# Layer 1's query projection as seven block products for eight, and another order for the slot

## The chip, the core and the metric

The kernel runs on one core of a Trainium2 chip as one launch. The metric is device time in microseconds of that launch, from several runs; one more execution was taken by the hardware profiler. PE is TensorE (PEld its weight loads), DVE VectorE, ACT ScalarE, POOL GpSimd, SP the engine whose queue issues most DMA transfers.

## What is computed

Two transformer layers with adaptive layer norm, on x of 2 x 512 x 512 (two batches b, 512 tokens, width 512), all in fp32. Layer 0 is a sliding-window attention and a low-rank-adapted FFN; layer 1 a latent attention with 128 heads and a routed FFN. The part that is changed is in layer 1's attention:

```python
    q_c = (c_q @ Wq_up).reshape(b, s, N_HEADS, HEAD_DIM)        # 4 per head
    q_r = (x @ Wq_rope).reshape(b, s, N_HEADS, ROPE)            # 64 per head; 512 x 8192 weights
    ...
    scores = (einsum('bqhd,bkhd->bhqk', q_c, k_c) + einsum('bqhd,bkd->bhqk', q_r, k_r)) / scale
    attn = softmax(scores)
    out = einsum('bhqk,bkhd->bqhd', attn, v_c)
    out = out.reshape(b, s, N_HEADS * HEAD_DIM) @ Wo
```

## The kernel before

Layer 0 comes first (to about 920 us of the profiled execution). Its loop runs over 64 steps, four for each of 16 units (8 key-value groups times 2 batches). In each step stand, in an order written out by hand, the scores of one block of 128 queries, the band and maximum on DVE, the exponentials on ACT, the normalisation on POOL, and block products for the next and the last unit. Layer 0's own query and output projections are already block products of half size (`ps_q` at L856, `pw` at L1002: 128x256 instead of 128x512). Into the steps is put, one piece a step, a list `aside`: the modulation rows of both layers, 21 pieces.

Layer 1's attention is a loop of 64 **slots**. A slot t is one of `quads`: a group g of 16 heads (of 8), a batch b, and a quarter s of the group; four heads as two pairs p = 0, 1. What a slot does:

- `query` (L1296): q of one pair of heads, `psq` = 128 rows (2 heads x 64) x 512 tokens, four matmuls over the input width; weights `wqr`, one 512 KB load per slot. `query_out` (L1306, ACT) copies it to SBUF.
- `inner`, `inner_hi`, `inner_parts` (L1315, L1326, L1333): the latent queries or keys of two slots; `own_query` (L1355) masks them for one pair, on POOL for p = 0 and on DVE for p = 1.
- `rope` (L1363, L1372): scores of one pair for 128 keys (block i of 4), `s`, 64-row matmuls, two heads side by side. `keep` (L1382, ACT) copies them to SBUF, `largest` (L1389, DVE) keeps the running maximum.
- `blocks`, `tops`, `twice`, `join`, `top`, `top_hi`, `top_lo`, `stripes`: the maximum over keys for each query, ending on POOL (L1432). `row` h (L1442) spreads it over 128 partitions with one 64-row matmul for each of the four heads into `psm`: heads 0 and 1 from partitions 0 to 63, heads 2 and 3 from 64 to 127. `row_copy` and `row_even` (L1454, L1458, ACT) take three of the four to SBUF.
- `less_even`, `less_odd` (L1463, L1465, L1469): the maximum subtracted; four on DVE straight from PSUM (head 0), twelve on POOL. `exponential` (L1472, ACT).
- `own_values` (POOL) and `mix` (L1518, PE): attention times values, 32-column matmuls into `acc`.
- `extra`, `extra_dve`, `extra_pool`: what is due once in four slots or so: values `psv`, the division `psb`, the output projection `psw`.

The order of all this is a table, `PLAN1`: each entry names an operation, its arguments and an offset in slots, and the loop issues them in that order; every engine takes its instructions in the order of issue. The tiles `psq`, `psu`, `psx`, `psm`, `psv`, `psb` and `psw` share three PSUM banks in rotation (`pX`); `s` has one buffer for each pair, `acc` one. After the loop `tail()` lists the last slot's rest and the FFN by hand; the dictionary `beside` places pieces of the FFN in the last slots.

Of the kernel before, what the change touches and what calls it, by code (L numbers as in the profile page):

```python
# [45 lines left out]
def adaln_kernel(ctx: ExitStack, tc: tile.TileContext, A: dict, out: bass.AP):  # L46
# [89 lines left out]
    def spread_gates(L, ws, g, pool, dst):  # L136

        n = 32 * len(ws)
        for i, s in enumerate(ws):
            for b in range(B) if s in dst else ():  # L140
                r = 32 * i + b
                ps = pool.tile([P, 512], F32, tag="mm", name=f"psg{L}_{s}_{b}")
                nc.tensor.matmul(
                    ps, lhsT=ident[:n, r : r + 1].to_broadcast([n, P]), rhs=g, start=True, stop=True
                )
                nc.scalar.copy(dst[s][b], ps)
# [138 lines left out]
    class Ffn1:  # L285
# [3 lines left out]
        def __init__(self, cp, wp, ap, pS, pX):  # L289
            self.cp, self.wp, self.ap, self.pS, self.pX = cp, wp, ap, pS, pX  # L290
            self.mv, self.rstd, self.xn, self.pl, self.pr, self.ps, self.hw = ({} for _ in range(7))
            self.wT, self.gate, self.gb = [], [], []
# [30 lines left out]
        def weight(self):  # L323

            h = len(self.wT)
            w = self.wp.tile([P, 2, D], F32, tag="wq", name=f"wT1_{h}")
            src = A["L1_ffn_WT"].rearrange("(kc p) o -> p kc o", p=P)
            nc.sync.dma_start(out=w, in_=src[:, 2 * h : 2 * h + 2, :])
            self.wT.append(w)

        def routes(self):
            nc.vector.tensor_copy(self.em, self.em_i)
            r = self.cp.tile([LAT, NH * HD1], F32, tag="wv", name="route")
            self.route = r[:N1, : E1 * R]
            nc.vector.tensor_scalar(self.route, self.erow, self.em, None, ALU.is_equal)

        def gates(self, b):
# [4 lines left out]
                lhsT=ident[:64, 32 + b : 33 + b].to_broadcast([64, P]),  # L342
# [4 lines left out]
            g = self.ap.tile([P, D], F32, tag=f"q{b}", name=f"g1_5_{b}")  # L347
# [3 lines left out]
        def low_weights(self):  # L351
            a = self.ap.tile([P, D], F32, tag="q0", name="aT1")
            self.aT = a.rearrange("p (kc e) -> p kc e", kc=KC)
            nc.sync.dma_start(out=self.aT, in_=A["L1_ffn_AT"].rearrange("(kc p) e -> p kc e", p=P))
            self.bT = self.ap.tile([P, D], F32, tag="q1", name="bT1")
# [174 lines left out]

    with ExitStack() as c01:
        mid = c01.enter_context(tc.tile_pool(name="mid", bufs=1, side="right"))
        gate = {2: gate_tiles(0, 2, state), 5: gate_tiles(0, 5, mid)}
        grow = [
            pool.tile([64, D], F32, tag=f"grow{L}", name=f"grow{L}")
            for L, pool in enumerate((mid, state))
        ]
        scs = [silu_c(L, mid) for L in range(2)]
        with ExitStack() as c00:
# [96 lines left out]
            def reload(t):  # L636
# [10 lines left out]
                ],  # L647
# [17 lines left out]
        attention1(tc, A, small, hT, xs, gate[2], ident, normalised, c01.close, Ffn1)  # L665
# [79 lines left out]
def attention0(  # L745
# [383 lines left out]
    tops 1 -2; extra_pool 1 -1; keep 0 0 -1; twice -2; keep 3 1 -2; join -2; own_query 1 0;  # L1129
    own_query 0 0; exponential 1 1 -3; rope 1 0 -1; respread -4; top -2; rope 0 1 -1; top_hi -2;  # L1130
    exponential 1 2 -3; top_lo -2; stripes -2; query_out 0 0; less_odd 1 3 -3; keep 0 1 -1;
    mix 1 -3; extra 0 0; row 3 -2; largest 1 0 -1; row 1 -2; keep 1 0 -1; rope 1 1 -1;
    row_copy 0 -2; rope 2 0 -1; extra_dve 0 0; own_values -2; row_copy 1 -2; row 2 -2;
    largest 1 1 -1; extra_pool 0 0; exponential 1 3 -3; less_odd 0 2 -2; row 0 -2;
    largest 2 0 -1; keep 1 1 -1; extra 1 0; less_even 0 2 -2; less_even 0 0 -2; mix 2 -3;
    keep 2 0 -1; less_odd 0 0 -2; mix 3 -3; less_odd 1 2 -2; row_even -2; rope 2 1 -1;
    rope 3 0 -1; inner -1; less_odd 1 0 -2; less_odd 0 3 -2; less_even 0 1 -2; less_even 1 0 -2;
    less_even 0 3 -2; largest 2 1 -1; exponential 0 2 -2; exponential 0 0 -2; inner_hi -1;
    largest 3 0 -1; keep 2 1 -1; less_even 1 1 -2; leave -3; extra_dve 1 0; less_odd 0 1 -2;
    keep 3 0 -1; query 1 1; inner_parts -1; blocks 0 -1; less_odd 1 1 -2; tops 0 -1;  # L1140
    exponential 1 0 -2; less_even 1 2 -2; rope 3 1 -1; exponential 0 3 -2; query_out 1 1;
    exponential 0 1 -2; less_even 1 3 -2; rope 0 0 0; largest 3 1 -1; mix 0 -2; query 0 1;
    blocks 1 -1;
# [3 lines left out]
def attention1(tc, A, small, hT, xs, ga, ident, normalised, close, ffn):  # L1147
# [17 lines left out]
    with ExitStack() as ctx:  # L1165
# [3 lines left out]
        def load_q(t):  # L1169
            g, _, s = quads[t]  # L1170
            w = wp.tile([P, KC, 2 * P], F32, tag="wq", name=f"wqr{t}")
            c0 = (4 * g + s) * 2 * P
            nc.sync.dma_start(out=w, in_=wqr[:, :, c0 : c0 + 2 * P])
            return w
# [35 lines left out]
        wv = cp.tile([LAT, NH * HD1], F32, tag="wv", name="wv")  # L1210
# [5 lines left out]
        wqs = {}  # L1216

        with ExitStack() as c:
# [28 lines left out]
            wqs[0] = load_q(0)  # L1247
            for b in range(B):
                normalised(b, pmm)
                for n, w in zip(names, downs):  # L1250
# [13 lines left out]
                    if n != "kr":  # L1264
                        nc.scalar.copy(hi[b][n], f)
                        nc.vector.tensor_sub(lo[b][n], f, hi[b][n].bitcast(F32))

# [7 lines left out]
        chain, later, last = [], [], []  # L1275
        todo = {(e, i): [] for e in ("dve", "pool") for i in range(2)}
# [15 lines left out]
        def query(t, pair):  # L1292
            b = quads[t][1]
            ps = hold["q", t, pair] = pX.tile([P, S], F32, tag="x", name=f"psq{t}_{pair}")
            for kc in range(KC):
                nc.tensor.matmul(  # L1296
                    ps,
                    lhsT=wqs[t][:, kc, pair * P : (pair + 1) * P],
                    rhs=hT[b][:, kc, :],
                    start=(kc == 0),  # L1300
                    stop=(kc == KC - 1),
                )

        def query_out(t, pair):
            q = qs[t, pair] = ap.tile([P, S], F32, tag=f"q{pair}", name=f"q{t}_{pair}")
            nc.scalar.copy(q, hold["q", t, pair])  # L1306

        def inner(t):
# [4 lines left out]
            ps = hold["u", n, i] = pX.tile([P, S], F32, tag="x", name=f"psu{n}_{i}")  # L1313
# [16 lines left out]
        def inner_parts(t):  # L1330
# [9 lines left out]
            )  # L1340

# [7 lines left out]
        def own_query(t, p):  # L1349
# [4 lines left out]
            e = nc.vector if p else nc.gpsimd  # L1354
            e.tensor_scalar_mul(c, src, cols[:, x : x + 1])  # L1355
# [54 lines left out]
        def join(t):  # L1410
            ps = hold["x", t] = pX.tile([P, P], F32, tag="x", name=f"psx{t}")
            nc.tensor.transpose(ps, ms[t].rearrange("p a b c -> p (a b c)"), ident)

        def top(t):
# [3 lines left out]
            nc.vector.tensor_reduce(m, src, AX.X, ALU.max)  # L1418

# [10 lines left out]
        def stripes(t):  # L1430
            m = hold["st", t] = ap.tile([P, 16, 32], F32R, tag="st", name=f"st{t}", bufs=2)
# [6 lines left out]
        def row(t, h):  # L1438

            ps = hold["m", t, h] = pX.tile([P, S], F32, tag="x", name=f"psm{t}_{h}")  # L1440
# [9 lines left out]
        def row_copy(t, p):  # L1450
# [3 lines left out]
            nc.scalar.copy(r, hold["m", t, 2 * p + 1])  # L1454

        def row_even(t):
            r = hold["r", t, 2] = ap.tile([P, S], F32, tag="rowe", name=f"rowe{t}", bufs=2)
            nc.scalar.copy(r, hold["m", t, 2])  # L1458

        def less_even(t, p, i):  # L1460
# [3 lines left out]
            else:  # L1464
                nc.vector.tensor_sub(s, s, hold["m", t, 2 * p])  # L1465
# [8 lines left out]
        def values(t):  # L1474
# [3 lines left out]
            def product():  # L1478
                ps = pX.tile([P, TB, 64], F32, tag="x", name=f"psv{t}")
# [10 lines left out]
            def copy(ps):  # L1490
                v = vcs[g, b] = ap.tile([P, TB, 64], F32, tag="v", name=f"v{t}")
                nc.vector.tensor_copy(v, ps)

# [32 lines left out]
        def leave(t):  # L1526
# [30 lines left out]
            def spreading():  # L1557
                ps = pX.tile([P, S], F32, tag="x", name=f"psb{g}_{b}")
# [3 lines left out]
            def scale(ps):  # L1562
# [4 lines left out]
                )  # L1567

# [3 lines left out]
            def project(i):  # L1572
                ps = pX.tile([P, 512], F32, tag="x", name=f"psw{G}_{b}_{i}")
# [5 lines left out]
            def gated(i, ps):  # L1579
                y = ap.tile([P, D], F32, tag="y", name=f"y1_{G}_{b}_{i}", bufs=2)  # L1580
                nc.vector.tensor_mul(y, ps, ga[b])
                return y
# [37 lines left out]
        def extra_pool(t, i):  # L1620
# [7 lines left out]
            for f in (  # L1628
                query, query_out, inner, inner_hi, inner_parts, respread, own_query, rope,
# [17 lines left out]
        F = ffn(cp, wp, ap, pS, pX)  # L1647
# [16 lines left out]
        beside = {  # L1664
# [245 lines left out]
```

## Time and profile before

| | us |
|---|---|
| runs | 2483.36 median of 3 (2481.84 to 2483.59) |
| the profiled execution | span 2480.0, its run 2481.8 |
| layer 0 and the start of layer 1 | 0 to about 920 |
| slots | about 920 to 2380 |
| last FFN | to 2480 |

Busy over the whole span: PE 97%, PEld 52%, DVE 74%, ACT 57%, POOL 71%. The stages differ, and the shares are to be read stage by stage. In the rows of the profile a group is named by line, engine, operation and tiles; "128*128" is the shape of PE's array that a matmul uses, "64*128" one half of its rows, "128*32" a quarter of its columns. A fp32 matmul shows as two instructions (two passes), one of type fp32r as one. A PE length includes some 0.16 us of pipeline, so that lengths overlap; what a pass costs is read from the distance of the starts.

### The profile page before, as it was taken

What the parts mean: (1) busy time and instruction counts of PE and PEld (TensorE: products, weight loads), DVE (VectorE), ACT (ScalarE), POOL (GpSimd) and SP (SyncE); (2) the same over time, 40 slices, a digit from 0 to 9 for tenths busy, and PEclk for the clock granted to TensorE, in tenths of its full rate; (3) what the DMA queues carried; (4) which work ended last, traced back from release to release, by engine and by line L of the source; (5) the groups of instructions that cost most, each with busy time, mean ns of one, the idle gap of its engine ahead of it and who ended that gap; (6) DMA issues with size and microseconds to landing.
All of it is one profiled execution on the core that took longest, in us unless ns stands there. A gap on an engine that the chain in (4) does not pass through costs nothing.

```text
span 2480.0 us, 31453 instructions
## 1 busy us (share of the span) xinstructions
PE 2403.0 (97%) x11516; PEld 1278.4 (52%) x11516; DVE 1827.2 (74%) x2464; ACT 1419.0 (57%) x2128; POOL 1763.1 (71%) x1659
## 2 busy tenths in 40 slices
PE   6999999999999999999999999999999999999878
PEld 4677777777776543444444344444344434444333
DVE  4666777777788347777787788778877777788764
ACT  1232222222222127888888788878888888888640
POOL 2555567557577325888898888888988898888743
PEclk8999999999999999999999999999999999999978
DMA  6212101100101100000000100000000000010000
GB/s 215 73 48 81 41 14 33 43 14 31 35 5 39 45 11 26 26 26 26 26 18 26 30 19 25 26 26 26 22 27 26 26 18 26 30 33 18 18 9 34
DMA packets 79845, 83.14 MB, mean 34 GB/s; under 512 B 7885, under 2 KB 69100, under 8 KB 79692
## 3 DMA queue, kind: packets, MB, share of 16 engines
q1 hardware_dynamic: 79548, 81.00, 10.5%
q8 instruction: 91, 1.49, 0.3%
q14 instruction: 62, 0.51, 0.1%
q0 software_dynamic: 144, 0.15, 0.0%
HBM read 79.03 MB, written 2.10 MB: 33 GB/s over the span
## 4 chain that ended last, share of the span: by engine, by line
PE 91%; DVE 5%; POOL 2%; ACT 1%; issue 1%; DMA 0%; SPq 0%; DVEq 0%; POOLq 0%; ACTq 0%
PE s L1363 19%; PE psq L1296 18%; PE acc L1518 10%; PE ps_q L856 7%; PE pw L1002 7%; PE s L1372 5%; PE po L951 4%; PE scores L898 2%; PE ps_k L797 2%; PE pt L940 2%; PE psv L811 2%; PE psu L1315 2%; PE psm L1442 2%; PE psw L1574 1%; PE psf L505 1%; PE psf L270 1%
## 5 line engine op out<-in xcount | busy, mean ns | idle before, releaser
L1469 POOL TENSOR_TENSOR ss<-ss,row 128x512 f32<-128x512 f32 x504 | 635.1, 1289 | 42.5 <-ACT row L1454 42.5
L1382 ACT COPY ss<-s 128x1024 f32<-128x1024 f32 x512 | 505.4, 1015 | 177.2 <-PE s L1372 130.6
L1363 PE MATMUL s<-q,ckr 64*128 64x512 f32 x2048 | 554.9, 612 | 10.5 <-ACT ss L1382 10.5
L1472 ACT ACTIVATE ss<-ss 128x1024 f32<-128x1024 f32 x512 | 525.2, 1070 | 5.7 <-DVE ss L1684 4.6
L1296 PE MATMUL psq<-hT,wqr 128*128 128x512 f32 x1024 | 467.2, 598 | 0.0
L1372 PE MATMUL s<-qm,c 64*128 64x512 f32 x1024 | 419.3, 795 | 0.4 <-DVE c L1333 0.4
L1389 DVE TENSOR_TENSOR mx<-s,mx 128x1024 f32<-128x1024 f32 x256 | 306.7, 1219 | 40.2 <-PE s L1372 39.2
L1463 POOL TENSOR_TENSOR ss<-ss,rowe 128x512 f32<-128x512 f32 x252 | 318.5, 1288 | 0.0
L1296 PEld LDWEIGHTS psq<-hT,wqr 128*128 128x128 f32 x1024 | 188.9, 189 | 241.0 <-issue 210.4
L1363 PEld LDWEIGHTS s<-q,ckr 64*128 64x128 f32 x2048 | 184.2, 186 | 215.1 <-ACT ss L1382 97.1
L1518 PE MATMUL acc<-ss,vp 128*32 128x512 f32 x2048 | 266.1, 612 | 0.0
L790 POOL TENSOR_TENSOR qT<-t_q,t_q 128x512 f32<-128x512 f32 x64 | 82.0, 1281 | 234.8 <-DVE t_q L789 234.8
L1389 DVE TENSOR_TENSOR mx<-s,ss 128x1024 f32<-128x1024 f32 x128 | 156.7, 1225 | 116.7 <-ACT row L1454 80.6
L942 ACT COPY pT<-pt 128x512 f32<-128x512 f32 x64 | 37.6, 587 | 229.7 <-PE pt L940 229.7
L1432 POOL TENSOR_TENSOR st<-mh,own_block 128x512 fp32r<-128x512 f32 x64 | 67.0, 1047 | 142.8 <-DVE mh L1428 142.8
L1372 PEld LDWEIGHTS s<-qm,c 64*128 64x128 f32 x1024 | 104.7, 187 | 119.0 <-issue 114.9
L1394 DVE STREAM_TRANSPOSE mx<-mx 128x1024 f32<-128x1024 f32 x128 | 158.8, 1241 | 2.3
L1400 DVE TENSOR_REDUCE m<-mx 128x32 f32<-128x1024 f32 x128 | 156.1, 1220 | 4.4
L1465 DVE TENSOR_TENSOR ss<-ss,psm 128x512 f32<-128x512 f32 x252 | 155.7, 680 | 0.0
L1355 POOL TENSOR_SCALAR qm<-c,cols 128x512 fp32r<-128x512 f32 x64 | 102.6, 1603 | 44.0 <-PE s L1372 24.7
L931 POOL TENSOR_TENSOR p<-p,rs 128x512 f32<-128x512 f32 (+1 forms) x64 | 108.6, 1697 | 26.8 <-DVE rs L930 22.6
L1518 PEld LDWEIGHTS acc<-ss,vp 128*32 128x32 f32 x2048 | 47.5, 109 | 138.0 <-issue 106.7
(249 smaller groups left out, 3906.1 us busy)
## 6 DMA issues: line engine op xcount, KB each, us to landing
wqr<-in_L_attn_Wq_rope_pairs SPq DMA_DIRECT2D x64, 512.0 KB
wmod<-in_L_wmod SPq DMA_DIRECT2D x20, 512.0 KB
wq<-in_L_attn_wq SPq DMA_DIRECT2D x8, 1024.0 KB
wo<-in_L_attn_wo SPq DMA_DIRECT2D x32, 256.0 KB
wmod<-in_L_wmod SPq DMA_DIRECT2D x2, 1024.0 KB
x<-in_L_attn_x SPq DMA_DIRECT2D x8, 256.0 KB
wk<-in_L_attn_wk SPq DMA_DIRECT2D x8, 256.0 KB
wv<-in_L_attn_wv SPq DMA_DIRECT2D x8, 256.0 KB
```

Source lines behind the costliest of these rows:

```text
L856: nc.tensor.matmul(ps[:, j, :], lhsT=s[:, k, j * P : (j + 1) * P], rhs=t[:, k, :], start=(k == 0), stop=(k == 1),)
L1002: nc.tensor.matmul(ps[:, j, :], lhsT=s[:, hh, j * P : (j + 1) * P], rhs=t[:, hh, :], start=(hh == 0), stop=(hh == 1),)
L1296: nc.tensor.matmul(ps, lhsT=wqs[t][:, kc, pair * P : (pair + 1) * P], rhs=hT[b][:, kc, :], start=(kc == 0), stop=(kc == KC - 1),)
L1363: nc.tensor.matmul(out[:, j, :], lhsT=whole[b]["kr"][r, bass.ts(i, P)], rhs=qs[t, p][r, :], start=True, stop=False,)
L1372: nc.tensor.matmul(out[:, j, :], lhsT=qkc[t // 2, 1][r, bass.ts(i, P)], rhs=qm[t, p][r, :], start=False, stop=True,)
L1382: nc.scalar.copy(ss[t, i, p], hold["s", t, i, p])
L1389: nc.vector.tensor_max(mx[t, p], hold["s", t, i, p], before)
L1394: nc.vector.transpose(m, m)
L1463: nc.gpsimd.tensor_sub(s, s, hold["r", t, 2])
L1469: nc.gpsimd.tensor_sub(s, s, hold["r", t, 2 * p + 1])
L1472: nc.scalar.activation(ss[t, i, p], ss[t, i, p], AF.Exp)
L1518: nc.tensor.matmul(accs[g, b][32 * h : 32 * (h + 1), :], lhsT=vps[t][:, kb, h, :], rhs=ss[t, kb, h // 2][:, h % 2, :], start=(s == 0 and k ...
```

## The change

The query projection of a slot, 256 outputs x 512 inputs times 512 x 512 tokens, is cut in 2 x 2 blocks and done as seven products of 128 x 256 x 256 (Strassen's scheme in Winograd's form). What it needs:

- Sums of weight blocks, S1, S2 and S4, for each of the 32 (g, s). `blending` makes them in layer 0 as 33 more pieces of `aside`, one a step: a 512 KB load, one DVE add of 128x512, two POOL adds of 128x256, and a 512 KB store into DRAM (`blended`, which holds a fourth, the unused first quarter, too).
- Sums of token blocks, once for each (g, b), `combine` on POOL (three of 128x512) into `part0` to `part2`; one more subtraction is made in place in hT at the start of layer 1.
- `product` j = 0 to 3 in place of `query`: one, two, two and two block products, each 2 matmuls of 128x256. Weights come as seven loads of 128 KB a slot into a ring of eight, each issued after the product that used its place.
- `sums` i = 0 to 5 in place of `query_out`: an ACT copy of 128x256, two DVE operations of 128x512, three of 128x256, each reading PSUM and SBUF.

`own_query` 0 goes from POOL to ACT. `PLAN1` is a new table; among others, the rows 1 and 0 now stand together, with row 2 and row 3 each between two `rope` entries of a pair, and both `extra` entries stand next to products 0 and 1. `stripes` and `row_even` have one buffer for two. `beside` is a list that also waits for a bank to be free; some operations of the last slots are left out of the loop since `tail()` issues them. The layer-1 gate rows, Wv_up and the routing table share one tile, and the FFN's weights go into the ring of the query weights.

```diff
+        def blend(i):
+            w = held.pop().rearrange("p k (r n) -> p r k n", r=2)
+            a11, a12 = (w[:, 0, 2 * k : 2 * k + 2, :] for k in range(2))
+            o = pool.tile([P, KC, DH], F32, tag="wmod", name=f"bo{i}", bufs=2)
+            _, s1, s2, s4 = (o[:, j, :].rearrange("p (k n) -> p k n", k=2) for j in range(KC))
+            nc.vector.tensor_add(
+                o[:, :2, :].rearrange("p j (k n) -> p j k n", k=2),
+                w[:, :, :2, :],
+                w[:, 1, :, :].rearrange("p (j k) n -> p j k n", j=2),
+            )
+            nc.gpsimd.tensor_add(s2, s1, a11)
+            nc.gpsimd.tensor_add(s4, s2, a12)
+            if i + 1 < len(blended):
+                load(i + 1)
+            nc.sync.dma_start(out=blended[i], in_=o)
...
-                ],
+                ] + blending(tmp),
...
-        def load_q(t):
-            g, _, s = quads[t]
-            w = wp.tile([P, KC, 2 * P], F32, tag="wq", name=f"wqr{t}")
...
+        def load_q(n):
+            t, k = divmod(n, 7)
...
+            nc.sync.dma_start(out=wq[:, n % 8, :, :], in_=src)
...
-        def query(t, pair):
-            b = quads[t][1]
-            ps = hold["q", t, pair] = pX.tile([P, S], F32, tag="x", name=f"psq{t}_{pair}")
-            for kc in range(KC):
-                nc.tensor.matmul(
...
+        def combine(t, j):
+            b = quads[t][1]
+            if quads[t][2] == 0:
+                nc.gpsimd.tensor_tensor(
+                    parts[j],
+                    parts[0] if j else quarter(b, 0, 1),
+                    quarter(b, (0, 1, 1)[j], (0, 1, 0)[j]),
+                    ALU.add if j else ALU.subtract,
+                )
+
+        def product(t, j):
+            b = quads[t][1]
+            ps = hold["q", t, j] = bank([P, 2, DH], f"psq{t}_{j}")
+            rhs = (
+                (quarter(b, 0, 0),),
+                (quarter(b, 1, 0), parts[0]),
+                (parts[1], quarter(b, 0, 1)),
+                (quarter(b, 1, 1), parts[2]),
+            )[j]
+            n = 7 * t + max(2 * j - 1, 0)
+            for i, r in enumerate(rhs):
+                for k in range(2):
+                    nc.tensor.matmul(
+                        ps[:, i, :],
+                        lhsT=wq[:, (n + i) % 8, k, :],
+                        rhs=r[:, k, :],
+                        start=(k == 0),
+                        stop=(k == 1),
+                    )
+            for m in range(n, n + len(rhs)):
+                if m + 8 < 7 * NQ:
+                    load_q(m + 8)
...
+            if i == 0:
+                nc.scalar.copy(q[:, 3, :], ps[:, 0, :])
+            elif i == 1:
+                nc.vector.tensor_add(q[:, 0::3, :], q[:, 3:4, :].to_broadcast([P, 2, DH]), ps)
+            elif i == 2:
+                nc.vector.tensor_sub(q[:, 1:3, :], q[:, 3:4, :].to_broadcast([P, 2, DH]), ps)
+            elif i == 3:
+                nc.vector.tensor_sub(q[:, 3, :], ps[:, 1, :], q[:, 1, :])
+            elif i == 4:
+                nc.vector.tensor_add(q[:, 1, :], q[:, 1, :], ps[:, 0, :])
+            else:
+                nc.vector.tensor_sub(q[:, 2, :], ps[:, 1, :], q[:, 2, :])
...
-            e = nc.vector if p else nc.gpsimd
-            e.tensor_scalar_mul(c, src, cols[:, x : x + 1])
+            if p:
+                nc.vector.tensor_scalar_mul(c, src, cols[:, x : x + 1])
+            else:
+                nc.scalar.mul(c, src, cols[:, x : x + 1])
```

The new table, with what bears on PE's order and the banks in it:

```diff
+    extra 1 0; rope 0 0 -1; rope 0 1 -1; less_even 1 0 -3; combine 1 0; own_values -2; twice -2;
...
+    exponential 0 2 -3; sums 2 0; own_query 1 0; rope 1 0 -1; rope 1 1 -1; sums 3 0; largest 1 0 -1;
+    exponential 1 2 -3; keep 1 0 -1; row 1 -2; row 0 -2; largest 1 1 -1; mix 2 -3; rope 2 0 -1;
+    row_copy 0 -2; keep 1 1 -1; less_even 1 3 -3; row 2 -2; rope 2 1 -1; extra_pool 1 -1;
+    exponential 1 3 -3; less_even 0 1 -2; combine 0 1; combine 2 0; keep 2 0 -1; less_even 0 3 -2;
+    largest 2 0 -1; largest 2 1 -1; mix 3 -3; keep 2 1 -1; row_even -2; extra_pool 0 0;
+    less_odd 0 3 -2; less_odd 0 0 -2; less_even 0 2 -2; less_even 0 0 -2; rope 3 0 -1; row 3 -2;
+    row_copy 1 -2; keep 3 0 -1; rope 3 1 -1; largest 3 0 -1; inner -1; inner_hi -1; less_odd 0 1 -2;
+    keep 3 1 -1; product 3 0; exponential 0 0 -2; blocks 0 -1; product 0 1; inner_parts -1;
+    sums 4 0; sums 5 0; less_odd 1 1 -2; largest 3 1 -1; less_even 1 1 -2; blocks 1 -1; product 1 1;
+    tops 1 -1; extra 0 0; leave -3; exponential 0 3 -2; sums 0 1; exponential 1 1 -2;
+    less_odd 1 0 -2; respread -1; tops 0 -1;
```

In the table of before, `row 3` and `row 1` stand together, and so do `row 2` and `row 0`.

## The prediction

> **What bounds the kernel now.** I read the busy time by stretch first, then PE's (TensorE's) order inside the stretch that holds the change, then the rows of the single operations. Durations are those of one profiled execution: span 2480.0 us, its run 2481.8, which is 1.6 below the median of the runs, 2483.36. The sum is made against 2481.8, and 1.6 is added at the end. About 0.2% (5 us) is what a measurement of this kernel can tell from no change.
>
> Busy time by stretch; the columns are the stretch, its length, busy us (and instructions) of PE, PEld, DVE, ACT and POOL, the clock, DMA:
>
> ```profile
> 0.00:920.00 920.00, 883.62 (x4524) 643.88 (x4525) 636.84 (x898) 210.17 (x686) 507.06 (x390) 0.99 0.15 48
> 1000.00:2300.00 1300.00, 1299.99 (x6150) 539.69 (x6148) 1026.34 (x1340) 1082.32 (x1290) 1123.67 (x1144) 1.00 0.08 25
> 2300.00:2480.00 180.00, 143.81 (x525) 61.67 (x523) 113.35 (x162) 73.30 (x90) 89.68 (x82) 0.85 0.05 18
> ```
>
> From 1000 to 2300, the loop over layer 1's slots, PE is busy 1299.99 of 1300 us at full clock; the others are at 79 to 86%. The stretch holds 58 slots (the once-a-slot rows count x58), so a slot takes 22.41 us, and it is as long as its PE work. The waits of PE in this stretch come out empty.
>
> PE's order in one slot (start, length of each merged group), and in layer 0 a run of passes half as wide:
>
> ```profile
> 1409.74 3.60 PE L1296 MATMUL psq<-hT,wqr 128*128 128x512 f32 x8
> 1413.27 1.13 PE L1363 MATMUL s<-q,ckr 64*128 64x512 f32 x4
> ...
> 1423.76 0.50 PE L1442 MATMUL psm<-st,own_head 64*128 64x512 f32 x2
> 1424.10 1.02 PE L1363 MATMUL s<-q,ckr 64*128 64x512 f32 x4
> ...
> 1426.28 0.39 PE L1442 MATMUL psm<-st,own_head 64*128 64x512 f32 x2
> 1426.60 1.92 PE L1518 MATMUL acc<-ss,vp 128*32 128x512 f32 x16
> ```
>
> ```profile
> 376.48 3.72 PE L856 MATMUL ps_q<-th,s 128*128 128x256 f32 x16
> 380.04 1.04 PE L940 MATMUL pt<-ident,p 128*128 128x128 f32 x8
> ```
>
> The eight 512-wide query passes hold PE from 1409.74 to 1413.27, 3.53 us. The single starts lie 0.429 apart, and the last step is 0.52 because the next group has another array shape (64 rows). A fp32 matmul is two passes, so a slot has 16 of these. In layer 0 sixteen 256-wide passes take 3.56 us, starts 0.216 apart and 0.10 more once. A change of array shape (128 rows; 64 rows; 32 columns) thus costs about 0.1 on leaving and 0.1 on the first pass after. The psm rows come in pairs: one pass in the lower 64 rows and one in the upper run together, 0.34 and 0.32 us a pair.
>
> **The change, part by part.**
>
> *Products (PE).* 16 passes of 0.429 = 6.86 us become 7 block products x 2 matmuls x 2 passes = 28 of 0.216 = 6.05. That is -0.82 a slot, times 64 = **-52.2 us**. The half-wide price is a row of this kernel, same shape and type, so I take it as it stands. Each pass also loads weights (PEld 0.189): under 0.216 it still hides, as it does in layer 0.
>
> *Row passes (PE).* The new order table issues psm 1 and psm 0 together, then psm 2 and psm 3 alone, each between two s groups. Rows 0 and 1 both sit in the lower 64 rows, 2 and 3 in the upper. So nothing is left to run as a pair: four passes one after the other, where there were two pairs. A pass is about 0.217 (a pair's 0.32 less a change), so +0.43 a slot; 63 slots use the table: **+27.3 us**. Bounds: 0 if the chip overlaps them with neighbours after all, 27.3 if not. I take 27.3, since an s group uses both halves.
>
> *Array changes (PE).* Counting along the built order of PE from the first s to the last table row, before has 602 changes of array shape, after 562: psw and psb now stand beside the query products instead of between psm and acc. 40 x 0.195 = **-7.8 us**. Counted this way (passes times step, plus changes), before gives 996.6 us over 44 slots where the trace has 992.7, so the counting itself is good to 0.4%.
>
> At one place a page speaks against all this. The Trainium skill, "TensorEngine Tiling (Array Packing)", section Instruction Overhead, gives each matmul some 60 cycles of overhead. At a clock of 2.4 GHz, which "TensorE: Matmul & The Clock Gate" states in its table, an estimate is 25 ns a pass, for 12 more passes +0.3 us a slot and +19 us in all, which would leave a gain of only 14. The trace disagrees: 0.216 against half of 0.429 is under 2 ns.
>
> *Reading the products (DVE, ACT).* Two ACT copies of psq (588 ns each, L1306) go; a 128x256 copy comes (a 64x256 copy from PSUM took 365). DVE gets five reads of PSUM plus SBUF: two 128x512 (0.68, the L1465 row) and three 128x256. These have no row: bounds 0.36 (half, and a little) and 0.68; I take 0.42, as the 128x256 copy at L1492 took 425. Together 2.6 us (at most 3.4). DVE has 1026.34/58 = 17.7 a slot; it comes to 20.3 (21.1) of 21.9. Its cover is thus 1.6 (0.8) us a slot: PE hides it, barely.
>
> ```profile
> L1465 DVE TENSOR_TENSOR ss<-ss,psm x232: 676/680/684, 1002.3 to 2282.5; 128x512 f32<-128x512 f32 x116
> ```
>
> ```profile
> L787 DVE TENSOR_TENSOR t_q<-qT,rope x51: 692/693/1753, 107.1 to 696.2; 128x512 f32<-128x512 f32 x51
> ```
>
> (ns, least/median/most.) The first has one operand in PSUM and never varies, with POOL 86% busy beside it. The second reads SBUF twice and sometimes takes 1.75. All five new reads are of the first kind.
>
> *POOL and ACT.* own_query 0 (1603 ns, L1355) goes from POOL to ACT, where a scaled 128x512 takes some 690 (L1326). POOL gets three combines of 1.29 per four slots, 0.97 each. POOL: 19.4 - 1.6 + 1.0 = 18.8 a slot; ACT: 18.7 - 1.18 + 0.37 + 0.69 = 18.6. Both under 21.9: 0.
>
> *The bank that is closest.* Three PSUM banks rotate over ten tiles a slot. psu takes the bank of psm 0, which is free after the fourth less_even on DVE. From the end of product 2, DVE has in its order: sums 2, own_query 1, sums 3, two largest, two less_even, two largest, two less_even = 0.62+0.5+0.36+2.28+1.24+2.28+1.24 = 8.5 us (steps between starts). PE, up to psu: two s groups 2.28, psm 0.53, acc 1.0, s 1.19, psm 0.22, s 1.19, acc 1.0, s 1.19, psm 0.22, s 1.19 = 10.0. DVE is 1.5 us early. Cost 0; with the cover gone, 64 us for each us late.
>
> *Weights.* 64 loads of 512 KB become 448 of 128 KB on SP, each waiting for the product eight loads back, about a slot ahead. Behind them in SP stand only the wo loads, needed slots later. DMA is at 0.08. Cost 0.
>
> *Layer 0.* 32 steps each get a load, a DVE add 128x512 of the L787 kind (0.69 to 1.75), two POOL adds 128x256 (about 0.64 each), and a store. DVE's add stands just before the band add, where DVE waited for PE 0.2 to 0.8 us, 0.5 on average. POOL is 63% busy. On SP the next load waits for POOL's second add; queued behind are wo, wk, wv and wq loads, which already waited long for their buffers:
>
> ```profile
> SPq L709 <- PE pw L1002: 251.9, 22, 54.0
> ```
>
> PE has no idle time here, but slack: t_q at 463.6 gave qT by 464.8, for scores at 467.4. Bounds: 0, and 32 x (1.75-0.5) = 40 us. I take **+3**.
>
> *Start and end of layer 1.* The in-place subtraction and first combine (2 x 1.29 on POOL) lie beside 12 matmuls, 10.3 us of PE. The tail is the same code: psf weights wait for the last product, some 70 us ahead of use. 0, within 3 either way.
>
> Sum: -52.2+27.3-7.8+3 = -29.7; 2481.8-29.7+1.6 = **2453.7**.
>
> **Rivals.**
> (1) *The row passes cost nothing*: -27.3 more, 2426. For it: pairs do overlap. Against: the halves don't fit. If only psm 2 and 3 hide, 2440.
> (2) *DVE gives its banks back late* (slower). Place: psu behind the fourth less_even. Price 64 us per us beyond 1.5; it decides no change from 2.0 late (1.5+0.5 gained). Two collisions of the 1.75 kind per slot (2 x 1.05 = 2.1) plus three reads at the upper bound on the way (+0.3) make 2.4: +58 us, 2511. Against: the L1465 row.
> (3) *Layer 0's covers are gone*, +40 instead of 3: 2490. For it: PE is at 100% there too, and DVE's new add is of the colliding kind. Against: 0.5 of wait in front of it.
> (4) *Something outside these*, start or tail, 2453 +- 30.
>
> **How the numbers follow.** Forecast 0.67 (2440 to 2470, faster). (1) 0.07, faster. (2) 0.14: 0.02 faster, 0.02 same, 0.10 slower, since it may be mild. (3) 0.08: 0.04, 0.02, 0.02. (4) 0.04: 0.01, 0.01, 0.02. Faster 0.81, same 0.05, slower 0.14. The range, 2438 to 2486: the low end leaves out rival 1 in full, the high end takes in most of (3) and leaves out (2).
>
> **What would show it.** PE still at 1300 of 1300 in the slots and a slot near 21.9; 0.216 steps in psq; single psm passes of 0.2 to 0.3; DVE near 92%; L1465's kin at 0.68. Wrong if PE waits on less_even, sums or inner_parts; if layer 0 ends later than before by more than 5 us; or if psm adds nothing.

## The result, and the profile after

The changed kernel takes 2718.24 us (median of 4 runs, 2716.68 to 2718.81); the kernel before took 2482.7 beside it. The ratio is 1.0948, 95% interval [1.0929, 1.0967]: slower by 235.5 us, where 29.7 faster was forecast. The profiled execution has a span of 2714.9 us, 234.9 more than before's.

Where the time went is read from two tiles that start once in a fixed place. The first line of each pair is the first weight product of layer 1 (its first start ends layer 0), the second the turn of the score maxima, once a slot. Before, then after:

```profile
L1253 PE MATMUL pscq<-hT,L_attn_Wq_down x16: 592/592/697, 889.1 to 909.7; 128*128 128x512 f32 x16
L1412 PE MATMUL psx<-ident,m x64: 272/273/476, 951.2 to 2374.0; 128*128 128x128 f32 x64
```

```profile
L1299 PE MATMUL pscq<-hT,L_attn_Wq_down x16: 592/592/697, 930.1 to 951.5; 128*128 128x512 f32 x16
L1517 PE MATMUL psx<-ident,m x64: 327/328/476, 991.4 to 2605.1; 128*128 128x128 f32 x64
```

Layer 0 ends 930.1 - 889.1 = 41.0 us later. From the first psx to the last it is 1613.7 us for 1422.8: 190.9 more in 63 slots, 3.03 a slot. From layer 1's start to the first psx it is 61.3 for 62.1, and from the last psx to the end 109.8 for 106.0. The four differences, 41.0, 190.9, -0.8 and 3.8, make 234.9. In the steady part (psx 10 to 58) a slot is 25.49 us, before 22.52; where a slot is named below, it is this one.

Busy time by stretch, the columns as in the prediction:

```profile
0.00:920.00 920.00, 854.96 (x4405) 628.38 (x4406) 642.20 (x891) 201.07 (x668) 555.09 (x437) 0.98 0.26 85
1100.00:2400.00 1300.00, 1160.58 (x6033) 596.61 (x6033) 1050.86 (x1442) 936.65 (x1136) 966.83 (x1000) 1.00 0.12 37
```

In layer 0 PE has 855.0 us in the first 920, where it had 883.6. In the slots, where it was busy 1299.99 of 1300 us, it now is 1160.58, at full clock; DVE is at 81%, ACT at 72, POOL at 74. No engine is the bound. So the slot is a chain of waits from engine to engine. PE's waits in that stretch, which came out empty before (us in total, times, longest):

```profile
PE s L1468 <- ACT ss L1487: 74.5, 101, 1.1
PE s L1468 <- DVE mx L1494: 39.5, 52, 0.8
PE psq L1374 <- DVE c L1435: 23.3, 51, 0.5
```

PE starts a new score tile s late because ACT's copy of the last one (keep, L1487) or DVE's maximum over it (largest, L1494) is late. The groups of these two say why; the last part of each line is the idle time ahead of them and what ended it:

```profile
L1487 ACT COPY ss<-s 128x1024 f32<-128x1024 f32 x409 | 412.0, 1020 | 353.0 <-DVE mx L1494 229.8 <-PE acc L1630 123.2
L1494 DVE TENSOR_TENSOR mx<-s,mx 128x1024 f32<-128x1024 f32 x206 | 246.8, 1219 | 198.7 <-ACT ss L1487 198.7
```

ACT stands 229.8 us for DVE, and DVE 198.7 us for ACT, over a tile that both only read. Before, the same two groups waited for PE:

```profile
L1382 ACT COPY ss<-s 128x1024 f32<-128x1024 f32 x464 | 457.9, 1015 | 147.3 <-PE s L1372 113.9 <-PE acc L1518 17.7 <-DVE mx L1389 15.7
L1389 DVE TENSOR_TENSOR mx<-s,mx 128x1024 f32<-128x1024 f32 x232 | 278.0, 1219 | 37.3 <-PE s L1372 36.2
```

The instruction order of the two programs shows what these waits are. An instruction's waits stand at its end; these are largest 2 0 on DVE before, then largest 2 0 on DVE and keep 2 1 on ACT after (slot numbers left out of the names). PE_49, DVE_49 and Activation_49 are the counters that PE, DVE and ACT raise as they finish instructions:

```
L1389 TensorTensor mx_0_8300<-s_2_0_8313,mx_0_8300 128x1024 [waits PE_49]
L1494 TensorTensor mx_0_8841<-s_2_0_8856,mx_0_8841 128x1024 [waits DVE_49,Activation_49]
L1487 TensorCopy ss_2_1_14836<-s_2_1_14820 128x1024 [waits DVE_49,Activation_49]
```

The count of ACT that largest 2 0 waits for is the one that keep 2 0 of the same tile brings, and the count of DVE that keep 2 1 waits for is that of largest 2 1; the other counter in each line is the engine's own. So the program has two engines read one score tile in turns, in the order in which the table issues them. Before's table always has largest ahead of keep. After's has keep ahead at tiles 2 0, 3 0 and 3 1 and largest ahead elsewhere. With one tile for each p, PE's next scores wait for both readers, one after the other. One slot in the timeline of DVE (start, length, and the wait in brackets):

```profile
1505.25 2.36 DVE L1494 TENSOR_TENSOR mx<-s,mx 128x1024 f32<-128x1024 f32 x2 [2.01 <-ACT ss L1487]
1507.52 1.28 DVE L1573 TENSOR_TENSOR ss<-ss,psm 128x512 f32<-128x512 f32 x2
1510.63 1.22 DVE L1494 TENSOR_TENSOR mx<-s,mx 128x1024 f32<-128x1024 f32 x1 [1.83 <-ACT ss L1487]
```

The copies of ACT and the score groups of PE beside them:

```profile
1504.19 1.02 ACT L1487 COPY ss<-s 128x1024 f32<-128x1024 f32 x1
1507.69 1.01 ACT L1487 COPY ss<-s 128x1024 f32<-128x1024 f32 x1 [2.48 <-DVE mx L1494]
```

```profile
1506.53 1.13 PE L1468 MATMUL s<-q,ckr 64*128 64x512 f32 x4 [0.76 <-DVE mx L1494]
1508.76 1.13 PE L1468 MATMUL s<-q,ckr 64*128 64x512 f32 x4 [0.64 <-ACT ss L1487]
```

ACT copies tile 2 0 from 1504.19 to 1505.21; only then does DVE read it (1505.25), and PE's scores 3 0 begin at 1506.53. DVE's maximum of 2 1 ends at 1507.61; only then does ACT copy it (1507.69), and PE's scores 3 1 begin at 1508.76. The wait passes from DVE to PE, to ACT and back to PE within 5 us, which is why no busy share is high.

Layer 0's loss is another wait, DVE's longest in 300 to 700 (us in total, times, longest):

```profile
DVE bo L551 <- DMA bl<-bo: 49.4, 15, 6.5
```

DVE's sum of one step waits until the store of the step before has landed, up to 6.5 us, and everything behind it on DVE is late. In one such step DVE's sum begins at 404.92, POOL reaches its second add only at 417.07, SP issues the store at 418.24, and DVE's next sum begins at 425.10, after 6.27 us of waiting.

### The profile page after: what moved, and what is told of

Same layout as the page of the kernel before. It is cut to its first block, busy times and chain, and to the rows that moved or that the text cites. A ratio compares the mean times of both kernels' runs of the same rounds, so it can differ in the third digit from the quotient of the medians.

```text
span 2714.9 us, 34328 instructions
## 1 busy us (share of the span) xinstructions
PE 2436.4 (90%) x12284; PEld 1435.3 (53%) x12284; DVE 2035.5 (75%) x2816; ACT 1401.2 (52%) x2128; POOL 1791.2 (66%) x1709
## 4 chain that ended last, share of the span: by engine, by line
PE 40%; DVE 28%; ACT 16%; issue 8%; POOL 6%; DMA 3%; SPq 0%; DVEq 0%; ACTq 0%; POOLq 0%
ACT ss L1487 11%; DVE mx L1494 9%; PE psq L1374 7%; PE ps_q L889 4%; DVE mx L1499 4%; PE acc L1630 4%; PE s L1468 4%; PE pw L1035 3%; DMA bl<-bo 2%; ACT row L1560 2%; PE po L984 2%; PE ps_k L830 2%; DVE q L1400 1%; DVE c L1435 1%; DVE m L1505 1%
## 5 line engine op out<-in xcount | busy, mean ns | idle before, releaser
L1487 ACT COPY ss<-s 128x1024 f32<-128x1024 f32 x512 | 515.6, 1020 | 437.2 <-DVE mx L1494 287.1
L1468 PE MATMUL s<-q,ckr 64*128 64x512 f32 x2048 | 569.6, 627 | 143.5 <-ACT ss L1487 92.7
L1494 DVE TENSOR_TENSOR mx<-s,mx 128x1024 f32<-128x1024 f32 x256 | 306.7, 1219 | 242.6 <-ACT ss L1487 242.6
L1468 PEld LDWEIGHTS s<-q,ckr 64*128 64x128 f32 x2048 | 171.3, 185 | 377.1 <-ACT ss L1487 192.4
L1571 POOL TENSOR_TENSOR ss<-ss,rowe 128x512 f32<-128x512 f32 x252 | 326.2, 1295 | 0.0
L1374 PE MATMUL psq<-hT,wq 128*128 128x256 f32 x1024 | 269.0, 385 | 27.8 <-DVE c L1435 27.8
L1374 PEld LDWEIGHTS psq<-hT,wq 128*128 128x128 f32 x1024 | 189.2, 190 | 78.2 <-DVE c L1435 52.3
L1374 PE MATMUL psq<-part,wq 128*128 128x256 f32 x768 | 198.2, 380 | 1.6 <-DVE q L1398 1.6
L1374 PEld LDWEIGHTS psq<-part,wq 128*128 128x128 f32 x768 | 144.2, 194 | 20.3 <-DVE q L1398 2.7
L1494 DVE TENSOR_TENSOR mx<-s,ss 128x1024 f32<-128x1024 f32 x128 | 149.8, 1209 | 0.1
L954 ACT ACTIVATE p<-scores,nm 128x256 f32<-128x256 f32 (+1 forms) x256 | 111.5, 454 | 30.0 <-DVE nm L944 27.1
```

What stands on the lines that cost most here:

```text
L1374: nc.tensor.matmul(ps[:, i, :], lhsT=wq[:, (n + i) % 8, k, :], rhs=r[:, k, :], start=(k == 0), stop=(k == 1),)
L1468: nc.tensor.matmul(out[:, j, :], lhsT=whole[b]["kr"][r, bass.ts(i, P)], rhs=qs[t, p][r, :], start=True, stop=False,)
L1487: nc.scalar.copy(ss[t, i, p], hold["s", t, i, p])
L1494: nc.vector.tensor_max(mx[t, p], hold["s", t, i, p], before)
L1571: nc.gpsimd.tensor_sub(s, s, hold["r", t, 2])
```

## The experiments

Theory A: the turns at the score tiles make the slot long. Theory B: DVE is late because it has 2.6 us a slot more to do. Theory C: the single row passes and row copies set the pace. Times are medians; the kernel before takes 2482 to 2483 in every comparison.

**turns.** Two entries of the changed kernel's table moved. Each engine still issues the same instructions in the same order; only the waits between ACT and DVE differ.

```
-combine 2 0; keep 2 0 -1; less_even 0 3 -2; largest 2 0 -1; largest 2 1 -1;
+combine 2 0; less_even 0 3 -2; largest 2 0 -1; keep 2 0 -1; largest 2 1 -1;
-row_copy 1 -2; keep 3 0 -1; rope 3 1 -1; largest 3 0 -1;
+row_copy 1 -2; rope 3 1 -1; largest 3 0 -1; keep 3 0 -1;
```

> The changed kernel with two entries of its order table moved: keep 2 0 stands behind largest 2 0, and keep 3 0 behind largest 3 0. No engine's own order changes by this, only which of ACT (keep) and DVE (largest) reads the score tile s first. Theory A (two engines that read the same score tile take turns in the order of the table; in the changed kernel DVE is made to wait for ACT at tiles 2 0 and 3 0, ACT for DVE at 2 1, and PE for both, since there is one tile for each p): DVE's 206 us of waits for ACT in 1350 us mostly go, a slot falls from 25.47 to 22.3 to 22.9 us, and the time from 2718 to about 2550 (2520 to 2570). Theory B (DVE is simply late, having 2.6 us more a slot to do): the order of two readers is nothing, slot 25.3 to 25.6, time within 10 us of 2718. Theory C (the single row passes and the row copies set the pace): same as B.

Measured 2569.47 us, slot 23.16: 148.8 us less, 2.33 a slot, for two entries. Its line of psx, to be read beside the changed kernel's above:

```profile
L1517 PE MATMUL psx<-ident,m x64: 327/328/476, 990.3 to 2463.1; 128*128 128x128 f32 x64
```

DVE's maxima no longer wait for ACT's copies at all; the groups in 1200 to 2300, and the stretch:

```profile
L1494 DVE TENSOR_TENSOR mx<-s,mx 128x1024 f32<-128x1024 f32 x192 | 234.7, 1223 | 17.1 <-PE s L1477 17.1
L1513 DVE COPY m<-m 128x64 f32<-128x64 f32 x47 | 56.2, 1195 | 1.6
```

```profile
1200.00:2300.00 1100.00, 1062.14 (x5618) 560.07 (x5611) 1029.33 (x1340) 876.86 (x1057) 905.59 (x932) 1.00 0.14 41
```

Theory A holds in kind and nearly in size (the slot is 0.3 longer than its range). What is new is that DVE is now busy 1029 of 1100 us, 21.7 us of a 23.16 us slot.

**before_turns.** The kernel before, with the two keeps moved the other way. Unlike in turns, ACT's own order changes with it: keep 2 0 now stands ahead of keep 1 1, and keep 3 0 ahead of keep 2 1.

```
-largest 2 0 -1; keep 1 1 -1;
+keep 2 0 -1; largest 2 0 -1; keep 1 1 -1;
...
-mix 2 -3; keep 2 0 -1;
+mix 2 -3;
...
-largest 3 0 -1; keep 2 1 -1;
+keep 3 0 -1; largest 3 0 -1; keep 2 1 -1;
...
-less_odd 0 1 -2; keep 3 0 -1;
+less_odd 0 1 -2;
```

> The kernel before, with its eight products and everything else, but keep 2 0 set ahead of largest 2 0, and keep 3 0 ahead of largest 3 0, as the changed kernel's table has them. Here ACT's copies stand later than DVE's maxima, so DVE must now wait. Theory A: slot from 22.4 to about 23.4, time about 2545 (2520 to 2570), with DVE's maxima waiting for ACT's copies. Theories B and C: 2483 within 5 us, since no instruction is added or moved on any engine.

Measured 2523.81 us, ratio 1.0166 [1.0146, 1.0186], slot 23.05. No work was added, and the kernel lost 41 us; DVE's waits for the copies `ss` came up from nothing (1000 to 2300; its waits put down to `row` are 71.2 us, 73.2 before):

```profile
DVE mx L1388 <- ACT ss L1381: 136.8, 114, 2.1
```

The direction is A's, the size two thirds of what was expected. A possible reason, not tested, is that before's table has more of PE's other work between the score tiles. Contrary to what was expected ahead of it, the edit does move instructions on ACT, so how much of the 41 us is the turns alone stays open; turns, which moves none, is the clean one of the two.

**thin_sums.** The sums of the seven products over 8 columns only, so that the rest of q stays zero (the first of the five shown).

```
-nc.vector.tensor_add(q[:, 0::3, :], q[:, 3:4, :].to_broadcast([P, 2, DH]), ps)
+nc.vector.tensor_add(q[:, 0::3, :8], q[:, 3:4, :8].to_broadcast([P, 2, 8]), ps[:, :, :8])
```

> The changed kernel with DVE's five sums a slot taken over 8 columns of each 128x256 block only (the rest of q stays zero): every instruction, wait and bank is kept, but DVE's 2.5 us a slot of sums shrink to about 0.8 or less. Theory A: the turns at the score tiles stay, the slot falls by less than 1 us, to 24.4 to 25.2, and the time to 2660 to 2700. Theory B (DVE's load is the cause): the slot falls by all that DVE is spared and more, to 23.5 or below, time 2600 or less.

Measured 2656.73 us (3 below A's range), slot 24.52. With DVE at 995 of 1300 us the slot is still 2.0 us above before's. So the load is not the first cause; it is worth about 1 us a slot while the turns are wrong.

**turns_act.** As turns, with own_query 1 on ACT.

```
-            if p:
-                nc.vector.tensor_scalar_mul(c, src, cols[:, x : x + 1])
-            else:
-                nc.scalar.mul(c, src, cols[:, x : x + 1])
+            nc.scalar.mul(c, src, cols[:, x : x + 1])
```

> The kernel 'turns' (keep 2 0 and keep 3 0 behind their largest), with own_query 1, a scaled 128x512 copy, on ACT where it was on DVE. In 'turns' DVE is busy 1029 of 1100 us, 21.7 us of a 23.16 us slot, with this copy at 1.07 us (0.57 before) and the 128x64 copy at 1.20 (0.40 before). If, with the turns put right, DVE's load is the second cause, taking 1.07 us from it shortens the slot by 0.4 to 1.0, to 22.2 to 22.8, time 2569 to about 2530 (2508 to 2545), and PE's 34 us of waits for ACT's copies in 1100 us shrink by half or more. If it is not DVE but ACT's copies or the banks, ACT has 0.7 us a slot more and the slot stays at 23.1 or grows, time 2565 or more.

Measured 2523.62 us, slot 22.47, 0.69 less, and PE's waits for ACT's copies fell from 33.8 to 4.5 us in 1100 (turns, turns_act, then the stretch):

```profile
PE s L1468 <- ACT ss L1487: 33.8, 48, 1.1
```

```profile
PE s L1465 <- ACT ss L1484: 4.5, 10, 0.5
```

```profile
1200.00:2300.00 1100.00, 1089.62 (x5799) 578.46 (x5797) 1021.89 (x1335) 933.59 (x1139) 926.20 (x962) 1.00 0.14 43
```

So DVE's load is the second cause. PE is at 99% again, and yet the slot is only 0.05 below before's, where the prediction had 0.5.

**no_blends, inplace, no_store.** Three variants of layer 0. no_blends leaves out the list of 32 sums. no_store leaves out the store's line. inplace writes the sums over the loaded tile:

```
+            nc.vector.tensor_add(a22, a21, a22)
+            nc.vector.tensor_add(a21, a11, a21)
+            nc.gpsimd.tensor_add(a11, a22, a11)
+            nc.gpsimd.tensor_add(a12, a11, a12)
...
+            nc.sync.dma_start(out=blended[i], in_=tile)
```

> The changed kernel without the 32 weight sums in layer 0: no loads, adds and stores there, and the seven products of layer 1 read slices of the raw weights in their place (so three of the seven have other data). Everything else as changed. If layer 0's part of the loss is the sums (the first product of layer 1 began at 930.1 us against 889.1 before, 41.0 later), it begins near 889 again and the time falls by 38 to 44 us, to about 2677. If part of it is the moved constants, tiles and banks around it, it falls by less. The slots stay at 25.4 to 25.5 us.

> The changed kernel with the weight sums of layer 0 made in place: DVE and POOL write the four blocks over the tile that was loaded, and that tile is stored; so the two tiles of the tag take turns as whole steps, and no add has to wait until the store of the step before has landed (it waits for a load instead, a step ahead). The same bytes move; DVE has two 128x256 adds where it had one of 128x512. Theory A for layer 0 (DVE, in order, stands at the add for the store of the one output tile, 49.4 us in the stretch 300 to 700, and the rest of DVE's work comes late to PE): the first product of layer 1 begins at 889 to 897 instead of 930, time 2718 less 33 to 41, so 2677 to 2685. Theory B (DVE's and POOL's added busy time, or the adds' collisions on SBUF, or the traffic): the adds are all still there, layer 1 begins at 920 or later, time above 2705. The slots stay at 25.4 to 25.6.

> The changed kernel with the 32 stores of the weight sums left out (the sums are still loaded and added; the products of layer 1 read slices of the raw weights, so three of the seven have other data). The first product of layer 1 began at 889.1 before, 930.1 in the changed kernel, 890.4 with no sums at all, 902.8 with sums in place. If the wait of DVE for the store is nearly all of layer 0's loss, it begins at 890 to 895 and the time is 2718 less 35 to 40; if the adds by themselves cost what 'inplace' still lost, at 898 to 906, and the time is 2718 less 24 to 32.

Layer 1 began at 890.4 with no sums (2674.46 us), at 902.8 with sums in place (2686.80) and at 908.2 without stores (2692.39), with the slot at 25.50, 25.49 and 25.51. The lines of the first two:

```profile
L1299 PE MATMUL pscq<-hT,L_attn_Wq_down x16: 592/592/697, 890.4 to 911.8; 128*128 128x512 f32 x16
```

```profile
L1295 PE MATMUL pscq<-hT,L_attn_Wq_down x16: 592/592/697, 902.8 to 924.2; 128*128 128x512 f32 x16
```

The first was as expected. inplace fell between its two theories, nearer to A (its time is 1.8 above A's range). no_store came out as the second of its two, with the time in that range and the start 2.2 above: taking the store's wait away gives 27.3 of the 41.0 us in one way and 21.9 in the other (there DVE waited 15.3 us in 300 to 700 for the loads instead). The rest is something else. These starts come from one profile each, and among programs with the same layer 0 they differ by some us: 930.1, 930.1, 928.1 and 934.5 in the changed kernel, turns, turns_act and thin_sums. So differences of 2 to 6 us between two of them are not certain.

**no_pool_adds, no_dve_adds.** inplace without the two last of the four lines above, and without the two first.

> The kernel 'inplace' without POOL's two adds a step in layer 0 (two of the four blocks are stored unsummed); loads, DVE's two adds and stores stay. 'inplace' still began layer 1 at 902.8, 13.7 us behind before, with PE waiting 6.5 us for POOL's oT and 5.0 for DVE's t_k in 300 to 700; taking a 690 ns copy from DVE ('tab31c') moved it by 0.8 only. If POOL's adds are what is left, layer 1 begins at 889 to 894 and the time is 2687 less 9 to 14. If DVE's are, it begins at 899 or later.

> The kernel 'inplace' without DVE's two adds a step in layer 0 (all four blocks are stored as POOL leaves them); loads, POOL's adds and stores stay. If POOL's adds are what is left, layer 1 begins at 898 or later; if DVE's 1.9 us of adds a step are, at 889 to 895 and the time is 2687 less 8 to 14.

Layer 1 began at 898.6 (2683.85 us) and 894.5 (2680.71): 4.2 us for POOL's adds and 8.3 for DVE's. Together 12.5, which is the 12.4 between inplace and no_blends. The times fell by less, 3.0 and 6.1 of 12.3 us. Both runs point to DVE's adds as the larger part of what was left (898.6 is just short of that reading's 899, 894.5 is in its range, though the time fell by less than its 8 to 14); the size of either part is no surer than the starts are.

**base, tab31, tab33, tab31b, tab31c.** Towards a version that keeps the seven products and beats both. base is turns_act and inplace together. tab31 and tab33 rearrange the table, tab31b moves one entry of tab31, and tab31c changes one copy of layer 0 in tab31b. First tab31's rows and scores, then the two small edits:

```
rope 1 0 -1; ... row 1 -2; row 3 -2; ... rope 1 1 -1; ... largest 1 0 -1; largest 1 1 -1; row_copy 0 -2; row_copy 1 -2;
mix 2 -3; row 0 -2; ... keep 1 0 -1; ... row 2 -2; keep 1 1 -1; rope 2 0 -1; ... rope 2 1 -1; largest 2 0 -1; largest 2 1 -1;
```

```
-rope 1 1 -1; respread -1; largest 1 0 -1;
+rope 1 1 -1; largest 1 0 -1;
...
-less_odd 1 0 -2;
+less_odd 1 0 -2; respread -1;
...
-                (nc.vector.tensor_copy if j else nc.scalar.copy)(pT, pt)
+                nc.scalar.copy(pT, pt)
```

> The kernels 'turns_act' and 'inplace' put together: both keeps behind their largest, own_query 1 on ACT, the sums of layer 0 made in place. If the three losses are separate, the time is 2523.6 less the 31.4 that 'inplace' saved (2718.2 less 2686.8): 2492 (2486 to 2498), still 0.4% above before: layer 1 begins 13 to 14 us late and the slot is 22.4 to 22.5, as before's 22.52. If they share a cause (a late layer 0 that a faster slot hides), it is below 2486.

> As 'base', with the order table rearranged: row 1 and row 3 stand together, and row 0 and row 2, so that each pair is one pass in the lower and one in the upper 64 rows; rope 2 0 and 2 1, and rope 3 0 and 3 1, stand together, with no psm or acc between them; every largest 1 to 3 stands ahead of its keep where that costs nothing. By the steps of 'turns_act' against before (psm 0.93 against 0.75 us a slot, s 9.69 against 9.27, acc 4.12 against 3.85, psq 6.15 against 7.06) the slot should fall by 0.3 to 0.7 to 21.8 to 22.2, and the time to 2447 to 2475: faster than both. If what is left in 'turns_act' is not PE's order but short waits for ACT and DVE, the gain is under 0.2 a slot and the time above 2480.

> As 'tab31', but only row 3 and row 0 stand together; row 1 stands alone between rope 2 0 and 2 1, and row 2 after the acc group. It has more slack for ACT and DVE ahead of the score tiles, and 0.1 to 0.3 us a slot more of row passes and array changes on PE than 'tab31'. If PE's steps decide, it is 5 to 20 us slower than 'tab31'; if the short waits decide, it is the same or faster.

> As 'tab31', with the entry respread moved to the end of the table, behind inner, whose copy of the key weights it overwrites; 'tab31' had it ahead, so one score term had the weights of the next group. It is a few short POOL copies in one slot of eight. Time as 'tab31', 2476 (2471 to 2481), so below before's 2482 by about 0.2%.

> As 'tab31b', with layer 0's second copy of the transposed probabilities (pT, 690 ns, 25 times in 300 to 700) on ACT where it was on DVE. In 'inplace' DVE was busy 357 of 400 us there, with 1.9 us of adds a step, and layer 1 still began 13.7 us late. If DVE's load is what is left, DVE falls by 17 in 400 us and layer 1 begins 5 to 12 us earlier, time 2465 to 2472; if POOL's adds are (75% busy, and PE waits for its oT), nothing changes, within 3 us of 'tab31b'.

base 2500.18, two above its range (slot 22.46, layer 1 from 905.6). tab31 2476.07, just above its range, slot 22.10 (one of its score terms has the weights of the next group, which tab31b puts right). tab33 2543.44, a miss by far: its slot is 23.13, 1.03 longer than tab31's, and half of that is PE's wait `psx <- DVE m`, 24.3 us in 1100, as the 128x64 copy on DVE took 1699 ns on average there; a copy that waits for POOL's instructions beside it (last section) was not in the working. The other half is not explained. tab31b 2478.91, in its range, ratio 0.9987 [0.9978, 0.9996]. tab31c 2475.92, ratio 0.9972 [0.9963, 0.9982]: faster than before by 6.2 us, 0.28%, where the prediction had 29.7, and than the changed kernel by 242. Its layer 1 began at 903.4, 0.8 earlier than tab31b's and not the 5 to 12 expected, so this copy on DVE was not what PE waited for, though taking DVE's adds away did help (8.3 us). The stretch that holds 1300 us of slots in tab31c:

```profile
1000.00:2300.00 1300.00, 1289.97 (x6976) 676.38 (x6976) 1176.80 (x1601) 1134.09 (x1374) 1100.23 (x1144) 1.00 0.15 44
```

PE is at 99%, with DVE at 91, ACT at 87 and POOL at 85: seven products do fit, in a table that is balanced for them.

## Why the prediction was wrong, by its steps

**That a slot is as long as its PE work.** This is the step that failed. It was true of before (1299.99 of 1300) and was carried over to another table after looking at one place only, "the bank that is closest", psu behind the fourth less_even. That place held: in 1100 to 2400 PE never waited for psu. The tiles that were closest are s, one for each p, with two readers. The prediction counted each engine's own order and load, and took the readers of a tile as free of each other. The order of the instructions with their waits, which is there before any run, would have shown DVE's maximum waiting for ACT's copy. Price: 2.33 us a slot (turns), of the 2.97 by which the slot grew (25.49 for 22.52; the prediction's 22.41 comes from taking 58 whole slots for the 1300 us). One of its own signs of being wrong did show, PE waiting for inner_parts, as the 23.3 us of `psq <- DVE c`; they were gone in turns, and so came from the turns, too.

**DVE's cover of 1.6 us a slot.** The new reads were priced right: 688, 675, 411, 422 and 418 ns in turns sum to 2.61 us a slot, where 2.6 was worked out. What was not priced is old work in new company. The 128x64 copy (396 ns on average before) takes 1195 in turns, and own_query 1 (574 before) takes 1070: 1.3 us a slot, most of the cover. The last section shows what they wait for. Rival 2 had the sign and the engine, but its place was psu and its collisions were the t_q kind; the price of 0.69 us a slot shows in turns_act. It is the second cause, not the first.

**Products.** The 28 steps of 0.216 held:

```profile
1510.62 1.03 PE L1374 MATMUL psq<-hT,wq 128*128 128x256 f32 x4
1511.48 1.03 PE L1374 MATMUL psq<-part,wq 128*128 128x256 f32 x4
```

From start to start 0.86 for four. Summing steps between starts over 32 slots of turns_act, psq takes 6.15 us a slot where it took 7.06: -0.92, forecast -0.82 without its changes of shape. No overhead per matmul shows, so the trace was rightly preferred to the rule (whose 19 us would have left 11 of the 29.7, not 14).

**Row passes and array changes.** Forecast +0.43 and -0.12 a slot. By the same sums psm takes 0.93 for 0.75, s 9.69 for 9.27 and acc 4.12 for 3.85: together +0.87. The count of shape changes came out (601 before and 563 after in the traces, for 602 and 562), but the rest was mis-sized. A score group that follows a lone psm pass starts slower than one that follows the other p's group, though both are 64 rows (in the changed kernel 0.56 us to its second half at 1503.41, and 0.46 at 1517.80); it was counted as no change of shape. In tab31b, with the rows paired and the groups together, psm is 0.77 and acc 3.85 again, but s is 9.56 and psq 6.26, so part is not explained by the pairing. In turns_act some of it are waits too short for the list of waits: the step from an acc group to the scores behind it is 0.52 us at the least and 0.64 on average, twice a slot, nearly all of acc's +0.27. The forecast of -32.7 us for the slots became about -3 with all long waits gone (0.05 x 63).

**Layer 0.** Forecast +3 within 0 and 40; it was 41.0, just over the upper bound. The working looked at the add's own length and at what SP's queue holds up behind the loads. It did not ask when the add may start. With two tiles in the tag, taken by loads and sums in turn, all sums use the same tile, so a sum waits for the store of the last one, and that store is issued only after POOL's second add, which POOL reached late. Price: 27.3 us (inplace), then 8.3 for DVE's adds, 4.2 for POOL's, 1.3 left, each to within a few us. Rival 3 named this size, with the adds' collisions as its cause; the adds, collisions or not, are the smaller part, so that its size came out was luck.

**Start and end, POOL, weights.** -0.8 and +3.8 us, the one within the 3 allowed and the other just beyond. PE has no wait for the weight loads among the long ones. POOL is not a bound.

## What to carry to other kernels

Where an order is written by hand, list for each single-buffered tile all that must happen between two of its writes, the turns of its readers included, and compare that chain with the writer's other work; the load of each engine does not show it. When work is added to an engine, price its old instructions again in their new company, too. When a tag's buffers are shared by loads and results, follow which buffer each gets.

## What the runs showed of the hardware that was not expected

PE's clock fell after waits well under 3 us. The same 16 passes in layer 0 of the changed kernel, without and with a wait of 2.36 us ahead (which itself follows one of 1.03, with 1.1 us of work between):

```profile
418.03 1.52 PE L931 MATMUL scores<-kT,qT 128*64 128x192 f32 x16
433.42 2.83 PE L931 MATMUL scores<-kT,qT 128*64 128x192 f32 x16 [2.36 <-POOL qT L823]
```

The stretch 430 to 440 had a granted clock of 0.66. Not each such wait did it: one of 2.21 us at 354.8 left the clock at 1.00, one of 2.03 at 664.5 took it to 0.83; and the slots, with 11% of PE idle in waits of at most 1.1 us, ran at 1.00. The Trainium skill, "TensorE: Matmul & The Clock Gate", section "HAM oscillation — how this bites in real kernels", states as the rule that PE should have no idle gaps above about 3.4 us. The measurement differs: shorter ones were enough here.

One and the same 128x64 copy on DVE took 1324 ns (median) in turns and 196 in the changed kernel, two programs that differ in two table entries only. First turns, then the changed kernel:

```profile
L1513 DVE COPY m<-m x64: 190/1324/1350, 990.0 to 2462.9; 128x64 f32<-128x64 f32 x64
```

```profile
L1513 DVE COPY m<-m x64: 189/196/921, 991.1 to 2604.9; 128x64 f32<-128x64 f32 x64
```

The Trainium skill, "SBUF — State Buffer", section "SBUF: two separate sides", describes a port pair that DVE and GpSimd hold in turn for a whole instruction. The traces agree for these copies. In turns 60 of the 64 took over 400 ns, and each of the 60 ends 48 to 56 ns after the end of one of POOL's instructions. In tab33 all 56 that took over 400 ns do, and the longest, 4446 ns, lasts until the fourth such end. own_query 1 in turns took over 600 ns 61 times of 64, and each time ends 280 to 300 ns after such an end. No run took POOL's work away from beside them.

Not tested: whether the chip would let ACT and DVE read one score tile at the same time. In every kernel here the program makes one wait for the other, and only the order of the two was changed.
